# Scan pass of a selective-scan, attention and FFN kernel: named buffers, y stored by pieces, and another order of work

## The chip, the cores and the metric

One core of a Trainium2 chip. The metric is the device time of one execution in microseconds. Before the change the median of three runs is 9894.99 us (9894.46 to 9900.35). The core has five engines that each work through their own list of instructions in order: PE (TensorE, matrix products and transposes into PSUM), DVE (VectorE), ACT (ScalarE), POOL (GpSimd) and SP (SyncE, which here issues almost all DMA transfers). They meet only in semaphores.

## The reference, cut to what matters

Layer 0 is a selective scan over an image of 64 x 64 positions, 8 batches, 192 inner channels, 16 states, run in four directions; layer 1 is an attention without softmax and a quantized feed-forward. The change touches the scan alone:

```python
def step(h, inps):
    d_t, u_t, b_t, c_t = inps
    h = h * jnp.exp(d_t[..., None] * A) + (d_t * u_t)[..., None] * b_t[:, :, None, :]
    y = jnp.einsum('bkdn,bkn->bkd', h, c_t)
    return (h, y)
...
y = out_y[:, 0] + inv_y[:, 0] + wh_y + invwh_y      # the four directions, flipped and transposed back
```

So for each batch, direction k, channel d and state n, `h` is a linear recurrence over 4096 positions; its input is delta x u x B, its decay exp(delta x A), and y sums C x h over the states and then over the directions.

## The kernel before, in words

Three passes run one after the other. The first (normalization, projections, convolution) ends and the second, the **scan pass**, begins at about 683 us; the third (output projection, attention, feed-forward) begins at about 9210 us.

**Tiles of the scan pass.** Batches go in 4 pairs. Each pair has three chunks of 128 partitions: c = 0 and 1 hold 128 channels of one batch (below: wide chunks), c = 2 holds the last 64 channels of both batches (mixed chunks). Each chunk goes through the four directions k, and each direction through 4 pieces of 1024 positions: 16 pieces to a chunk, 192 in all. Directions 2 and 3 run backwards over the positions. A piece has 16 states, and for each state n:

- `decay` (L720): ACT makes `da` = exp(A x delta).
- `products` (L759): the input of the recurrence, a [128, 1024] tile `wide` in PSUM (two of the eight banks), in one of three ways. For states that `WAYS` (L55) gives to ACT, `scaled` (L730) multiplies the transposed `duT` by B on ACT into `x` and PE transposes it into `wide`. For those given to POOL, `scaled_by_pool` (L746) does so on POOL into `xg`. For the rest PE spreads a row of `xb` (B) over the partitions into `wide` and DVE multiplies it in place by `du`.
- `scan` (L783): DVE runs the recurrence from `da` and `wide` into half of a tile `h` (two states to a tile), starting from `carry` unless the piece is the first of its direction.
- `carries` (L807): ACT copies the last column of both halves of `h` for the next piece. `times_c` (L822): POOL multiplies `h` by the loaded rows `c`. `sum_over_n` (L836): PE transposes and adds the terms into `acc` in PSUM.
- Once to a piece, `take_acc` (L878) has ACT copy `acc` into the tile `y`; after the last piece of directions 2 and 3, `store_y` (L894) sends the whole of `y` (4096 positions) to memory. For odd directions each part goes in two transfers.

Around these, `deltas_of` (L645) makes `delta` for two pieces, `prepare` (L596) loads `xb` and `u` and makes `bT`, `du` and `duT`. The projected delta, bT and duT pass through `wide` buffers too: PE fills one, ACT copies it out. `late_x_projection` (L678) and `late_split` (L700) do left-over work of the first pass during the scan.

**What sets the order.** Everything is a Python generator that yields (engine, cost, delay, buffers) before each step. `weave` (L148) is a planner: it keeps a clock for each engine, opens so many units of each kind at once (`room` in its call, L935), and each time emits the step that can begin first by its costs, ties broken by a rank (`at * N + n - lead`, where `lead` is the number in each `add` call). `InOrder` (L85, L93 records every operation) then pins that order on each engine, so the costs decide the order of the instructions, and the chip runs it with its own times. `keep_busy` (L583) adds filler matmuls of a zero tile where the planner sees PE idle.

**Buffers.** The scan pass has 4 `da`, 3 `h`, 4 `x`, 1 `xg`, 6 `c`, 3 `wide` and 1 `acc` buffers (L556). A pool hands its buffers out in turn: the n-th tile of a kind lies in the buffer of the tile n - count before, and waits until that one is released. `Slots` tells the planner the same thing.

Of the kernel before, what the change touches and what calls it, by code (L numbers as in the profile page):

```python
# [42 lines left out]
P = 128  # L43
# [8 lines left out]
NPC = L // T  # L52
NT = T // P

WAYS = [([4, 6, 7, 9, 10, 12, 14, 15], [2, 11]), ([3, 8, 9, 12, 14, 15], [2, 6, 13])]  # L55
NS = 3
SOFT = 2

# [73 lines left out]
class Slots:  # L132
# [5 lines left out]
    def when(self):  # L138
# [2 lines left out]
            return None  # L141
        return 0.0 if self.taken < self.count else self.ends.get(self.taken + 1 - self.count)

    def release(self, which, end):
        self.ends[which] = end


def weave(units, room, finished, between=None):  # L148

    free, clock = {}, 0.0
    waiting = {kind: [u for u in units if u[0] == kind] for kind in room}
    opened, ended, active = {kind: 0 for kind in room}, {kind: set() for kind in room}, []
    while True:  # L160
        for kind, todo in waiting.items():
            while opened[kind] < len(todo) and (opened[kind] < room[kind] or opened[kind] - room[kind] in ended[kind]):
                _, rank, unit = todo[opened[kind]]
                active.append([clock, rank, kind, opened[kind], unit, next(unit)])
                opened[kind] += 1
        best = None
        for at in active:
# [12 lines left out]
        at = best[1]  # L180
        engine, cost, delay = (*at[5], 0.3)[:3]
        if len(at[5]) > 3:
            at[5][3].taken += 1
        clock = best[0][0]
        if between is not None:
            between(engine, clock - free.get(engine, 0.0))
        free[engine] = clock + cost
        at[0] = clock + cost + delay
        try:
            at[5] = at[4].send(at[0])  # L190
        except StopIteration:
            active.remove(at)
            ended[at[2]].add(at[3])
# [47 lines left out]
    return (a_neg, dsum, dt_b, dt_w, sel, sel2), load_dt_w  # L241


def split(engines, pool_of, cost, src, row, rows, pieces, at, dst):

    act, pool, sp = engines
    wide, used = GRP, rows * pieces
    yield "sp", 0.7, 4.0
    bq = pool_of.tile([P, wide], F32, name="bq", tag="late2")
    src = src[row : row + rows].rearrange("r (s t) -> (r s) t", s=pieces)  # L250
    sp.dma_start(bq[0:used], src[:, at : at + wide])
    yield "act", 0.6
    bs = pool_of.tile([P, NS, wide], BF16, name="bs", tag="late")
    act.copy(bs[0:used, 0, :], bq[0:used])
    yield "pool", cost
    pool.tensor_sub(bq[0:used], bq[0:used], bs[0:used, 0, :])
    yield "act", 0.6
    act.copy(bs[0:used, 1, :], bq[0:used])
    yield "pool", cost
    pool.tensor_sub(bs[0:used, 2, :], bq[0:used], bs[0:used, 1, :])  # L260
# [13 lines left out]
def pass1(ctx, tc, g, load_dt_w, ident, mhalf, engines, w_xp, u_d, z_d, xd_d, b_d, dt_d):  # L274
# [254 lines left out]
    for pair in range(NB // 2):  # L529
        batches = (2 * pair, 2 * pair + 1)  # L530
        for b in batches:
            units += [("stats", statistics(b, q)) for q in range(NG)]
            units.append(("norm", group_norm(b)))
            units += [("proj", projection(b, q)) for q in range(NG)]
        for c in ORDER:
            units.append(("conv", convolution(pair, c)))
        for b in batches:
            for o in range(2 if b < LATE_X else 0):
                units += [("xproj", x_projection(b, o, q)) for q in range(NG)]
                if b < LATE:  # L540
                    units += [("split", after(("xd", b, o), split((act, pool, sp), two, 4.4, xd_d[b][o], *w))) for w in splits(b, o, b_d, dt_d)]
    units.append(("later", later_loads()))
    room = {"later": 1, "proj": 4, "norm": 1, "stats": 3, "xproj": 4, "split": 2, "conv": 3}
    weave([(kind, (list(room).index(kind), i), unit) for i, (kind, unit) in enumerate(units)], room, done)
# [3 lines left out]
def pass2(ctx, tc, g, ident, engines, fixed, w_xp, u_d, xd_d, b_d, dt_d, y_d):  # L548
# [5 lines left out]
    two = ctx.enter_context(tc.tile_pool(name="p2two", bufs=2))  # L554
    three = ctx.enter_context(tc.tile_pool(name="p2three", bufs=SOFT + 1))
    room = {"da": 4, "h": 3, "x": 4, "xg": 1, "c": 6, "wide": 3, "acc": 1}  # L556
    slots = {name: Slots(count) for name, count in room.items()}
    pools = {
        name: ctx.enter_context(tc.tile_pool(name=f"p2{name}", bufs=count, **({"space": PSUM} if name in ("wide", "acc") else {})))
        for name, count in room.items()  # L560
    }
    pieces = [
        (pair, c, k, NPC - 1 - i if k >= 2 else i) for pair in range(NB // 2) for c in range(3) for k in range(K) for i in range(NPC)
# [6 lines left out]

    def take(name, shape, dtype=F32):

        return pools[name].tile(shape, dtype, name=name), slots[name].taken

    def one_more(key, of, end):
        counts[key] = counts.get(key, 0) + 1
# [101 lines left out]
    def late_x_projection(b, o, q):  # L678

        yield "scans", 0  # L680
        pair, j = b // 2, b % 2
        cols = slice(q * GRP, (q + 1) * GRP)
        yield "sp", 1.8, 4.0
        ux = one.tile([P, 2, GRP], F32, name="ux", tag="late")
        sp.dma_start(ux[:, 0, :], u_d[b][o][0:P, cols])
        for i in range(2):
            sp.dma_start(ux[64 * i : 64 * i + 64, 1, :], u_d[2 * pair + i][o][P:DI, cols])
        yield "pe", 1.5, 0.2, slots["wide"]
        px, slot = take("wide", [P, T])
        for i, ty in enumerate((0, 1 + j)):  # L690
            pe.matmul(px[:, 0:GRP], w_xp[:, ty, o, :], ux[:, i, :], start=i == 0, stop=i == 1)
        end = yield "act", 0.58, 0.2
        xd = one.tile([P, GRP], F32, name="xd", tag="late2")[0 : 2 * NXD]
        act.copy(xd, px[0 : 2 * NXD, 0:GRP])
        slots["wide"].release(slot, end)
        end = yield "sp", 0.7, 3.0
        sp.dma_start(xd_d[b][o][:, cols], xd)
        one_more(("xd", b, o), NG, end)

    def late_split(b, o, which):  # L700

        yield "scans", 0
        if b >= LATE_X:
            yield "xd", b, o
        yield from split((act, pool, sp), one, 1.25, xd_d[b][o], *which)
        one_more(("split", b), 6, 0.0)

    def load_c(at, m):
# [11 lines left out]
    def decay(at, n):  # L720

        _, c, k, _ = pieces[at]
        yield "delta", at
        end = yield "act", 1.05, 0.2, slots["da"]
# [34 lines left out]
    def products(at, n):  # L759
# [11 lines left out]
        else:  # L771
# [6 lines left out]
            end = yield "dve", 1.22, 0.1  # L778
# [99 lines left out]
    def take_acc(at):  # L878
        pair, c, k, pc = pieces[at]
        o = k % 2  # L880
        yield "sum", at
        end = yield "act", 0.95, 0.1
        if at % (K * NPC) == 0:
            for i in range(2):
                ys[i] = one.tile([P, NBLK, P], F32, name=f"y{i}")
        acc, slot = made["acc"]
        dst = ys[o][:, pc * NT : (pc + 1) * NT, :]
        act.copy(dst, acc)
        slots["acc"].release(slot, end)
        if k >= 2 and at % NPC == NPC - 1:  # L890
            yield "sp", 7.5, 6.0
            store_y(ys[o], o, chunk_rows(pair, c))

    def store_y(y, o, parts):  # L894
        for part, b, ch in parts:
            if o == 0:
                sp.dma_start(y_d[b][0].rearrange("(i p) d -> p i d", p=P)[:, :, ch], y[:, :, part])
            else:

                rows = y_d[b][1].rearrange("(h i w) d -> w h i d", w=2, h=HH)  # L900
                for w in range(2):
                    sp.dma_start(rows[w][:, :, ch], y[w * HH : (w + 1) * HH, :, part])

    units = []
    for at, (pair, c, k, pc) in enumerate(pieces):
# [3 lines left out]
            units.append((kind, at * N + n - lead, unit))  # L909

        if at == 0 or at % SOFT == 1:
            add("soft", 14, deltas_of(at))
        add("prep", 12, prepare(at))
        for n in range(N):
            if n % 2 == 0:
# [7 lines left out]
            add("scan", 0, scan(at, n), n)  # L923
            if n % 2 == 1:
                if at % NPC < NPC - 1:
                    add("carry", 0, carries(at, n // 2), n)
                add("term", -2, times_c(at, n // 2), n)
                add("sum", -6, sum_over_n(at, n // 2), n)
        add("acc", 0, take_acc(at), N)
    late_x = [(b, o, q) for b in range(LATE_X, NB) for o in range(2) for q in range(NG)]  # L930
    late = [("split", 3 * N * (i + 1), late_x_projection(*which)) for i, which in enumerate(late_x)]
    last = [(b, o, w) for b in range(LATE, NB) for o in range(2) for w in splits(b, o, b_d, dt_d)]
    late += [("split", 5 * N * (i + 1), late_split(*which)) for i, which in enumerate(last)]
    units += sorted(late, key=lambda unit: unit[1])
    weave(units, {"soft": 1, "prep": 1, "c": 1, "da": 2, "x": 1, "xg": 1, "dbu": 2, "scan": 2, "carry": 1, "term": 1, "sum": 1, "acc": 1, "split": 1}, done, keep_busy)  # L935


@with_exitstack
# [301 lines left out]
```

## Time and profile before

The profiled execution took 9906.51 us, with a span of 9904.5 us from the first instruction to the last; the median of the timed runs is 9894.99 us.

| engine | busy us | share of the span | what it does most (from the groups of the page) |
|---|---|---|---|
| DVE | 9325.3 | 94% | 3072 scans, 5255.7 + 1703.1 us; 1216 products, 1462.4 us |
| ACT | 9119.9 | 92% | 14336 of x, 4198.0 us; 3072 of da, 3501.1 us |
| POOL | 9004.1 | 91% | 1536 products with c, 6962.1 us at 4554 ns |
| PE | 7951.6 | 80% | sums into acc 3165.9 us, transposes into wide 1523.3 + 495.4 us, filler 1066.0 us |

The granted TensorE clock is 0.963 over the span. One DMA queue carries 2109 MB. The y stores of the page are 8 of 2 MB, 24 of 1 MB and 16 of 512 KB.

How to read it: a busy share is an average over three passes and over both kinds of chunks, which have different limits. Back-to-back instructions of DVE overlap by some 0.085 us in the records, so the mean length of a group (2330 ns for a scan with carry) is longer than the rhythm in which they follow each other. The line L93 is the recording helper's, so instructions are told apart by their tiles.

### The profile page before, as it was taken

What the parts mean: (1) busy time and instruction counts of PE and PEld (TensorE: products, weight loads), DVE (VectorE), ACT (ScalarE), POOL (GpSimd) and SP (SyncE); (2) the same over time, 40 slices, a digit from 0 to 9 for tenths busy, and PEclk for the clock granted to TensorE, in tenths of its full rate; (3) what the DMA queues carried; (4) which work ended last, traced back from release to release, by engine and by line L of the source; (5) the groups of instructions that cost most, each with busy time, mean ns of one, the idle gap of its engine ahead of it and who ended that gap; (6) DMA issues with size and microseconds to landing.
All of it is one profiled execution on the core that took longest, in us unless ns stands there. A gap on an engine that the chain in (4) does not pass through costs nothing.

```text
span 9904.5 us, 162493 instructions
## 1 busy us (share of the span) xinstructions
PE 7951.6 (80%) x57093; PEld 6231.6 (63%) x57093; DVE 9325.3 (94%) x6971; ACT 9119.9 (92%) x21486; POOL 9004.1 (91%) x2911
## 2 busy tenths in 40 slices
PE   7768888888887887888888888878878878878787
PEld 3336666666666666666666666666666666666676
DVE  7879999999999999999999999999999999999687
ACT  5769999999999999999999999999999999999797
POOL 1449999999999999999999999999999999999677
PEclk8889999999999999999999999999999999999898
DMA  5776776789986776799976766899867667999663
GB/s 165 236 224 214 227 238 219 232 216 212 217 225 214 227 228 218 225 219 208 212 227 213 229 222 218 226 209 207 222 218 225 222 213 227 215 209 206 189 185 107
DMA packets 937134, 2120.70 MB, mean 214 GB/s; under 512 B 275371, under 2 KB 423628, under 8 KB 934786
## 3 DMA queue, kind: packets, MB, share of 16 engines
q1 hardware_dynamic: 933514, 2108.96, 76.1%
q8 instruction: 456, 7.47, 0.3%
q14 instruction: 356, 2.92, 0.1%
q0 software_dynamic: 432, 0.94, 0.0%
q10 hardware_dynamic: 2376, 0.40, 0.0%
HBM read 1934.36 MB, written 175.66 MB: 213 GB/s over the span
## 4 chain that ended last, share of the span: by engine, by line
ACT 28%; DVE 25%; issue 19%; PE 11%; POOL 8%; DMA 7%; SPq 1%; DVEq 0%; POOLq 0%; ACTq 0%
DVE h L93 18%; ACT x L93 12%; ACT da L93 10%; POOL c L93 6%; DVE wide L93 5%; PE wide L93 4%; PE acc L93 3%; DMA c<-xd_d 3%; PE pa L93 1%; ACT L93 1%; PE px L93 1%; PE mm L93 1%; DVE u L93 1%; DMA xb<-b_d 1%; ACT y L93 1%
## 5 line engine op out<-in xcount | busy, mean ns | idle before, releaser
L93 POOL TENSOR_TENSOR c<-c,h 128x2048 f32<-128x2048 f32 x1536 | 6962.1, 4554 | 177.7 <-DVE h L93 129.8
L93 DVE TENSOR_TENSOR_SCAN h<-da,carry,wide 128x1024 f32<-128x1024 f32 x2304 | 5255.7, 2330 | 147.7 <-PE wide L93 103.9
L93 ACT ACTIVATE x<-duT,bT 128x128 f32<-128x128 f32 (+1 forms) x14336 | 4198.0, 368 | 13.6 <-PE wide L93 12.3
L93 ACT ACTIVATE da<-delta,a_neg 128x1024 f32<-128x1024 f32 x3072 | 3501.1, 1144 | 139.8 <-DVE h L93 135.6
L93 PE MATMUL acc<-ident,c 128*128 128x128 f32 x24576 | 3165.9, 279 | 380.9 <-POOL c L93 366.7
L93 PEld LDWEIGHTS acc<-ident,c 128*128 128x128 f32 x24576 | 2811.3, 143 | 777.3 <-POOL c L93 649.2
L93 PE MATMUL wide<-ident,x 128*128 128x128 f32 x11264 | 1523.3, 280 | 483.5 <-DVE h L93 449.9
L93 DVE TENSOR_TENSOR_SCAN h<-da,wide 128x1024 f32<-128x1024 f32 x768 | 1703.1, 2268 | 59.0 <-PE wide L93 37.1
L93 PEld LDWEIGHTS wide<-ident,x 128*128 128x128 f32 x11264 | 1268.1, 143 | 768.0 <-DVE h L93 331.9
L93 DVE TENSOR_TENSOR wide<-du,wide 128x1024 f32<-128x1024 f32 x1216 | 1462.4, 1209 | 91.3 <-PE wide L93 66.8
L93 PE MATMUL acc<-sel,zero 96*128 96x512 bf16 x3941 | 1066.0, 380 | 0.0
L93 PE MATMUL wide<-xb,sel 96*128 96x512 bf16 x2432 | 733.2, 386 | 291.8 <-DVE h L93 277.1
L93 POOL TENSOR_TENSOR xg<-duT,bT 128x512 f32<-128x512 f32 (+1 forms) x640 | 892.7, 1409 | 24.1 <-PE wide L93 12.1
L93 PE MATMUL wide<-ident,xg 128*128 128x128 f32 x3584 | 495.4, 284 | 162.4 <-DVE h L93 155.8
L93 PEld LDWEIGHTS <-zero 96*128 96x128 bf16 x3941 | 383.2, 98 | 304.8 <-issue 5.5
L93 PEld LDWEIGHTS wide<-ident,xg 128*128 128x128 f32 x3584 | 416.3, 146 | 249.5 <-issue 149.2
L93 PEld LDWEIGHTS <-sel 96*128 96x128 bf16 x2432 | 220.8, 99 | 458.0 <-issue 226.7
L93 POOL TENSOR_TENSOR du<-delta,u 128x1024 f32<-128x1024 f32 x192 | 457.2, 2381 | 41.2 <-DMA u<-u_d 20.9
L93 DVE SCALAR_TENSOR_TENSOR u<-xpad,conv_w,u 128x4096 f32<-128x4096 f32 x96 | 451.2, 4700 | 1.9
L93 ACT COPY carry<-h 128x2 f32<-128x2 f32 x1152 | 214.4, 186 | 139.9 <-DVE h L93 134.2
L93 POOL TENSOR_TENSOR bq<-bq,bs 128x512 f32<-128x512 f32 (+1 forms) x48 | 120.2, 2506 | 172.1 <-ACT bs L93 163.5
L93 ACT ACT_TABLE_LOAD x196 | 251.5, 1283 | 22.9 <-DMA b2q_raw<-in_b 19.4
(150 smaller groups left out, 6239.5 us busy)
## 6 DMA issues: line engine op xcount, KB each, us to landing
c<-xd_d SPq DMA_DIRECT2D x1024, 1024.0 KB
c<-xd_d SPq DMA_DIRECT2D x1024, 512.0 KB
u<-u_d SPq DMA_DIRECT2D x127, 512.0 KB
xdt<-dt_d SPq DMA_DIRECT2D x1146, 36.0 KB
xb<-b_d SPq DMA_DIRECT2D x382, 96.0 KB
u<-u_d SPq DMA_DIRECT2D x128, 256.0 KB
zs<-z_d SPq DMA_DIRECT2D x128, 256.0 KB
y_d<-y SPq DMA_DIRECT2D x24, 1024.0 KB
```

The costliest lines, as they stand in the source:

```text
L93: ins = getattr(self.engine, op)(*args, **kwargs).ins
```

## The change

The arithmetic stays. What differs:

- Each buffer of the scan pass gets a name of its own (a tag in a pool of one buffer), and the planner's `Buffers` gives a new tile the buffer that comes free first, not the one whose turn it is. The numbers of buffers stay.
- `y` is stored after every piece of directions 2 and 3, a quarter at a time, in place of once after their last piece.
- Other states go to ACT and POOL in `WAYS`, as many as before to each (8 and 2 in wide chunks, 6 and 3 in mixed ones).
- Three products and three scans may be open at once in the planner (two before).
- Ranks: deltas 12 ahead in place of 14, carries 4 later, the copy of acc 2 later. Some costs and delays of the planner are other numbers (da 1.06 for 1.05; late transfers 12 and 25 us for 3 to 4; the delay behind DVE's product 0.0 for 0.1).

```diff
-WAYS = [([4, 6, 7, 9, 10, 12, 14, 15], [2, 11]), ([3, 8, 9, 12, 14, 15], [2, 6, 13])]
+WAYS = [([2, 4, 5, 9, 10, 13, 14, 15], [6, 12]), ([6, 7, 9, 12, 14, 15], [4, 8, 13])]
...
+class Buffers:
+    def __init__(self, count):
+        self.free, self.taken, self.held = [0.0] * count, None, False
+    def when(self):
+        return None if self.held else min((end for end in self.free if end is not None), default=None)
+    def take(self):
+        self.taken = self.free.index(self.when())
+        self.free[self.taken] = None
+    def release(self, which, end):
+        self.free[which] = end
...
-    slots = {name: Slots(count) for name, count in room.items()}
+    slots = {name: Buffers(count) for name, count in room.items()}
     pools = {
-        name: ctx.enter_context(tc.tile_pool(name=f"p2{name}", bufs=count, **({"space": PSUM} if name in ("wide", "acc") else {})))
-        for name, count in room.items()
+        name: ctx.enter_context(tc.tile_pool(name=f"p2{name}", bufs=1, **({"space": PSUM} if name in ("wide", "acc") else {})))
+        for name in room
     }
...
-        return pools[name].tile(shape, dtype, name=name), slots[name].taken
+        which = slots[name].taken
+        return pools[name].tile(shape, dtype, name=name, tag=f"{name}{which}"), which
...
-        yield "sp", 1.8, 4.0
+        yield "sp", 1.8, 12.0
...
-        end = yield "sp", 0.7, 3.0
+        end = yield "sp", 0.7, 25.0
...
-        yield from split((act, pool, sp), one, 1.25, xd_d[b][o], *which)
+        yield from split((act, pool, sp), one, 1.25, 12.0, xd_d[b][o], *which)
...
-        end = yield "act", 0.95, 0.1
+        end = yield "act", 0.95, 3.0
...
-        dst = ys[o][:, pc * NT : (pc + 1) * NT, :]
-        act.copy(dst, acc)
-        slots["acc"].release(slot, end)
-        if k >= 2 and at % NPC == NPC - 1:
-            yield "sp", 7.5, 6.0
-            store_y(ys[o], o, chunk_rows(pair, c))
+        of = slice(pc * NT, (pc + 1) * NT)
+        act.copy(ys[o][:, of, :], acc)
+        slots["acc"].release(slot, end - 3.0)
+        if k >= 2:
+            yield "sp", 3.0, 6.0
+            store_y(ys[o], o, of, chunk_rows(pair, c))
...
-                sp.dma_start(y_d[b][0].rearrange("(i p) d -> p i d", p=P)[:, :, ch], y[:, :, part])
+                sp.dma_start(y_d[b][0].rearrange("(i p) d -> p i d", p=P)[:, of, ch], y[:, of, part])
...
-            add("soft", 14, deltas_of(at))
+            add("soft", 12, deltas_of(at))
...
-                    add("carry", 0, carries(at, n // 2), n)
+                    add("carry", -4, carries(at, n // 2), n)
...
-        add("acc", 0, take_acc(at), N)
+        add("acc", -2, take_acc(at), N)
...
-    weave(units, {"soft": 1, "prep": 1, "c": 1, "da": 2, "x": 1, "xg": 1, "dbu": 2, "scan": 2, "carry": 1, "term": 1, "sum": 1, "acc": 1, "split": 1}, done, keep_busy)
+    weave(units, {"soft": 1, "prep": 1, "c": 1, "da": 2, "x": 1, "xg": 1, "dbu": 3, "scan": 3, "carry": 1, "term": 1, "sum": 1, "acc": 1, "split": 1}, done, keep_busy)
```

More of the change, by code (lines that the diff above doesn't have):

```diff
@@ L142, in when, with take @@
         return 0.0 if self.taken < self.count else self.ends.get(self.taken + 1 - self.count)
+    def take(self):
+        self.taken += 1
     def release(self, which, end):
         self.ends[which] = end
+class Buffers:
[3 more added lines that the diff above has]
+        return None if self.held else min((end for end in self.free if end is not None), default=None)
+    def take(self):
+        self.taken = self.free.index(self.when())
+        self.free[self.taken] = None
+    def release(self, which, end):
+        self.free[which] = end
 def weave(units, room, finished, between=None):
@@ L182, in weave @@
         if len(at[5]) > 3:
-            at[5][3].taken += 1
+            at[5][3].take()
         clock = best[0][0]
@@ L241, in scan_constants, with split @@
     return (a_neg, dsum, dt_b, dt_w, sel, sel2), load_dt_w
-def split(engines, pool_of, cost, src, row, rows, pieces, at, dst):
+def split(engines, pool_of, cost, landing, src, row, rows, pieces, at, dst):
     act, pool, sp = engines
     wide, used = GRP, rows * pieces
-    yield "sp", 0.7, 4.0
+    yield "sp", 0.7, landing
     bq = pool_of.tile([P, wide], F32, name="bq", tag="late2")
@@ L540, in pass1 @@
                 if b < LATE:
-                    units += [("split", after(("xd", b, o), split((act, pool, sp), two, 4.4, xd_d[b][o], *w))) for w in splits(b, o, b_d, dt_d)]
+                    units += [("split", after(("xd", b, o), split((act, pool, sp), two, 4.4, 4.0, xd_d[b][o], *w))) for w in splits(b, o, b_d, dt_d)]
     units.append(("later", later_loads()))
@@ L723, in decay @@
         yield "delta", at
-        end = yield "act", 1.05, 0.2, slots["da"]
+        end = yield "act", 1.06, 0.2, slots["da"]
         da, slot = take("da", [P, T])
@@ L777, in products @@
                 pe.matmul(dbu[:, q : q + GRP], spread(n, c), xb[:, q : q + GRP], start=True, stop=True)
-            end = yield "dve", 1.22, 0.1
+            end = yield "dve", 1.22, 0.0
             dve.tensor_mul(dbu, made[at][2], dbu)
@@ L886, in take_acc, with store_y @@
         acc, slot = made["acc"]
[L887 to L894 removed]
+        of = slice(pc * NT, (pc + 1) * NT)
[4 more added lines that the diff above has]
+            store_y(ys[o], o, of, chunk_rows(pair, c))
+    def store_y(y, o, of, parts):
         for part, b, ch in parts:
             if o == 0:
[L897 removed]
+                sp.dma_start(y_d[b][0].rearrange("(i p) d -> p i d", p=P)[:, of, ch], y[:, of, part])
             else:
@@ L901, in store_y @@
                 for w in range(2):
-                    sp.dma_start(rows[w][:, :, ch], y[w * HH : (w + 1) * HH, :, part])
+                    sp.dma_start(rows[w][:, of, ch], y[w * HH : (w + 1) * HH, of, part])
     units = []
```

## The prediction

> **What bounds the kernel now.** I read the busy shares of the page first, then a table of windows cut at the first scan of each chunk of the scan pass, then the waits of VectorE, then three places in the timeline. The page gives DVE 94%, ACT 92%, POOL 91%, so no share alone says who ends last. The table cut by chunk does; here are two chunks of pair 2, the first of the wide kind (128 channels of one batch), the second of the mixed kind (64 and 64 channels of two batches).
>
> ```profile
> core 0: us, PE busy (x) PEld busy (x) DVE busy (x) ACT busy (x) POOL busy (x), PEclk, DMA share, GB/s
> ...
> 5664.30:6358.60 694.30, 570.38 (x4302) 460.00 (x4300) 681.06 (x353) 657.34 (x1465) 675.64 (x178) 0.98 0.70 221
> 6358.60:7090.10 731.50, 590.08 (x4286) 471.42 (x4285) 700.26 (x369) 716.47 (x1957) 712.28 (x240) 0.96 0.94 211
> ```
>
> A wide chunk is held by DVE (681 of 694 us) with POOL close behind (676); a mixed chunk is held by ACT (716 of 731) with POOL at 712, and its DMA engines are 94% busy against 70%. Summed over the table's twelve rows: the eight wide chunks take 5589.9 us with DVE busy 5450.6 and POOL 5434.4; the four mixed ones take 2935.7 us with ACT busy 2856.8. The change leaves every count of arithmetic instructions as it is, so the most that an order can give in the pass is 139.3 + 78.9 = 218 us.
>
> Who ends DVE's gaps:
>
> ```profile
> DVE h L93 <- PE wide L93: 140.9, 105, 9.7
> DVE wide L93 <- PE wide L93: 66.8, 64, 4.2
> ```
>
> Total us, times, longest: DVE waits for products to arrive in PSUM. There are two kinds of such waits. The first, from the timeline of all engines (start, length, engine, work; in brackets the idle time before and who ended it):
>
> ```profile
> 7897.28 4.56 DVE L93 TENSOR_TENSOR_SCAN h<-da,carry,wide 128x1024 f32<-128x1024 f32 x2
> ...
> 7901.90 1.09 PE L93 MATMUL wide<-ident,x 128*128 128x128 f32 x8 [1.21 <-DVE h L93]
> ...
> 7903.13 2.35 DVE L93 TENSOR_TENSOR_SCAN h<-da,carry,wide 128x1024 f32<-128x1024 f32 x1 [1.28 <-PE wide L93]
> ```
>
> PE could only refill a PSUM buffer when the scan that read it ended at 7901.84, and DVE had no other work ready: 1.09 us of transposes plus two handoffs is the 1.28. I call this a tight refill. Undisturbed, the scan with carry repeats every 2.24 us and the product every 1.11. The second kind, from the DMA queue's timeline and then that of all engines:
>
> ```profile
> 9032.16 8.23 SPq L93 DMA_DIRECT2D y_d<-y  x2
> ```
>
> ```profile
> 9089.29 0.38 PE L93 MATMUL wide<-sel,xb 96*128 96x32 bf16 x8 [7.06 <-DMA xb<-b_d]
> ...
> 9091.59 2.35 DVE L93 TENSOR_TENSOR_SCAN h<-da,carry,wide 128x1024 f32<-128x1024 f32 x1 [9.69 <-PE wide L93]
> ```
>
> Two y stores of 1 MB each enter the queue, the c loads behind them fall due all at once, and 50 us later PE, DVE and ACT (7.00) all stand for one xb load behind that traffic.
>
> **The change, part by part.** The two orders of instructions can be counted without running anything. For each DVE operation I took the PSUM buffer of its product and counted the DVE operations between the one that freed this buffer and itself; the gaps come from the trace of before, as the time beyond the usual overlap of 0.085 us.
>
> 1. Tight refills (nothing between). Wide chunks: 56 before, mean 1.06 us, 59.6 us in all; the new order has 16. That removes 40 x 1.06 = 42.6 us. The naming of buffers is what allows it: before, a new product takes the buffer whose turn it is, now the one that comes free first.
> 2. A scan directly after the product that writes its own input loses 0.20 us (30.6 us over 152 cases in wide chunks); 70 are left: 82 x 0.20 = 16.4.
> 3. One operation between: 689 to 511 cases at 0.031 us: 5.5.
> 4. Against it: delta, bT and duT also pass through these buffers (PE fills, ACT copies out, PE refills). Under the old turn such a buffer came back late. I count refills after such a passage with at most 5.7 us of DVE work to cover it: 38 before, 242 after. The passage of duT takes 1.04 (fill) + 1.00 (copy) + 1.07 (refill) and handoffs of 0.1 each, 3.4 us, that of bT 1.9 to 2.4; against covers of mostly 4.5 and 5.6 it is hidden, with one microsecond of slack. The nearest row: the 38 old ones lost 10.4 us, 0.27 each. So between 0 and 204 x 0.27 = 55 us; I take 15, because 32 of the 38 lost under 0.3.
>
> Wide chunks: -42.6 - 16.4 - 5.5 + 15 = -49.5, leaving 5540 us, in which POOL's 5434 is 98.1%: possible, but near.
>
> 5. y by pieces. In piece 13 of the four mixed chunks DVE stood 6.3, 5.2, 6.6 and 9.7 us, each some 50 us after the stores of one direction's y, and 7.3 us in piece 1 of the first mixed chunk, 60 us after the last stores of the chunk before. Bytes and packet sizes stay; the burst becomes four of a quarter, about 45 us apart. I take 30 of the 35.1 us.
>  The skill speaks against this edit: "DMA: Bandwidth & Descriptors", sections "Anatomy of one DMA" and "Bandwidth", puts about 2.0 us of fixed cost on each DMA and asks for transfers of 1 MiB or more. There are 144 more y stores (192 for 48), of 128 to 512 KB: by the rule an estimate of 144 x 2.0 = 288 us of queue time. The row: SP's queue waits 5686.0 us of the pass for PE to free a c buffer, and nobody but the end of the pass waits for a y store to land. So I count 0 here. Each piece's store now also waits on SP for ACT's copy, with c loads queued behind it; six c buffers are some 27 us of scans, which hides a wait of a few us.
> 6. Mixed chunks: tight refills 20 to 14 at 1.26, own-product scans 61 to 34 at 0.257: 14.5 us. ACT holds these chunks, so I take half, 7.
> 7. Late splits are given 12 and 25 us for their transfers where they had 3 to 4: DVE stood once for such a tile (6.3 us behind POOL's bs). I take 5, between 0 and 15.
> 8. End of the pass:
>
> ```profile
> 9221.65 1.01 ACT L93 COPY y<-acc 128x1024 f32<-128x1024 f32 x1 [20.32 <-PE acc L93]
> 9222.69 7.16 SPq L93 DMA_DIRECT2D y_d<-y  x4
> 9229.89 2.83 SPq L997 DMA_DIRECT2D hmask<-in_head_mask  x1
> ...
> 9233.35 0.40 SPq L93 DMA_DIRECT2D y<-y_d  x1
> ```
>
> The last store takes SP 10.7 us from the copy's end to the first load of the output pass. With a quarter of the bytes, four issues near 0.45 and three of 0.4 us: 3.7. Gain 7.
>
> 9. At nothing: carry copies ranked four later. ACT stands 134 us for them, but in wide chunks ACT has 35 to 40 us spare; the reader of a carry comes a whole piece (about 43 us) later, and h is kept anyway by POOL's product of 4.55 us. If that cover goes, h comes free late and DVE waits. Also at nothing: delta asked for two states later, 155 more filler matmuls on PE (0.38 each, put where PE idles), other states per engine (8 and 2, 6 and 3, as before). ACT gets 113 more separate waits ahead of da: an issue step in the chain is 0.05, so 5.6 us, 2 of them in mixed chunks.
>
> Sum: -49.5 - 30 - 7 - 5 - 7 + 2 = **-97 us**. The profiled span of 9904.5 becomes 9808 (its run, 9906.5, becomes 9810); the median of the runs, 9895.0, lies 11 below that run and becomes 9798.
>
> On the bubbles of the first kind "Perfetto Trace Analysis", "Optimization Strategy", says that a gap repeating on the engine that should be full can mean too few buffers. By that rule nothing of items 1 and 6 would come, since there are three wide buffers before and after: the sum would be -46, 9849. The row says something else: most refills from the same three buffers lose nothing (689 cases with one operation between lost 0.031 each), so the place of the refill in the order decides, and the counts in the new order are what I go by.
>
> **The rivals.** *POOL takes over* (22%): POOL's c products are 4.55 us with 243 us of waits in the pass, 130 of them for DVE's h. If the others stay, DVE's recovered time turns into waits for h buffers, and half of 1 to 3 and of 5 is kept: -50, 9845. For it: POOL is 16 us per chunk from DVE. Against it: the same three h buffers now let many pieces through in 42.6 to 42.8 us, DVE's own work.
> *More than the counts* (20%): all of 5, 6 and 7 and most of the 139 us in wide chunks, since a lost microsecond on DVE also delays ACT and POOL: -155, 9740.
> *Nothing* (5%): gaps are only moved; about 9890.
> *Slower* (7%): item 4 goes wrong. PE and ACT are in-order, so a late ACT copy of duT or delta holds PE at the refill, and the sums behind it hold c buffers and SP. The other items sum to -112; with 242 short refills the kernel is slower once each loses over 0.5 us. At 0.7 each: +169 - 10 - 112 = +47, 9942. For it: one old case of it lost over 4 us. Against it: the slack of a microsecond.
>
> **How the numbers follow.** The forecast has 46%, with 9760 to 9835 as its own range. A difference under 0.2% (20 us) can't be told from none. Range 9715 to 9872: it takes in the first two rivals and leaves out nothing and slower. Faster 88%, same 5%, slower 7%.
>
> **What would show it.** In the profile after: DVE's waits for PE's wide from 208 to about 120 us; the wait of 5 to 10 us in piece 13 of each mixed chunk gone, with xb gone from PE's waits; wide chunks near 692 us on average, mixed ones near 725; SP from the last copy to the first y load under 5 us; ACT's waits for carry mostly gone. I am wrong if DVE's waits move to wide fills that follow duT, delta or bT, or if POOL shows gaps that DVE does not end.

## The result, and the profile after

The changed kernel takes 9725.8 us (median of 4 runs, 9717.4 to 9731.5) against 9897.7 us before on the same chip: ratio 0.9825, 95% interval 0.9808 to 0.9842. That is 172 us, where 97 were forecast. The time lies 34 us beyond the forecast's own range (9760 to 9835) and inside the whole range. The profiled execution has a span of 9728.5 us, 176 less than before. Cut at the first scan of each chunk, as before, its table of windows gives for the same two chunks (time, then busy us of PE, its weight loads, DVE, ACT, POOL, then the granted clock and the DMA share):

```profile
core 0: us, PE busy (x) PEld busy (x) DVE busy (x) ACT busy (x) POOL busy (x), PEclk, DMA share, GB/s
...
5571.40:6252.20 680.80, 563.61 (x4298) 448.46 (x4297) 678.71 (x353) 655.61 (x1463) 675.06 (x177) 1.00 0.73 226
6252.20:6969.90 717.70, 587.15 (x4317) 454.07 (x4316) 699.19 (x370) 710.54 (x1948) 709.97 (x240) 0.99 0.96 215
```

The wide chunk is now DVE's own work: 678.7 of 680.8 us. The mixed chunk is 7 us above ACT's. Summed by kind:

| | before | after | difference | forecast |
|---|---|---|---|---|
| eight wide chunks | 5589.8 | 5474.8 | -115.0 | -49.5 |
| four mixed chunks | 2935.8 | 2891.3 | -44.5 | about -37 |
| from the last scan to the end | 695.4 | 679.5 | -15.9 | -7 |

The waits of DVE, in total us, times and longest, within the scan pass (from 690 us, to leave out its first instructions):

```profile
DVE h L93 <- PE wide L93: 62.1, 45, 5.7
DVE wide L93 <- PE wide L93: 24.7, 26, 1.9
```

and those of ACT:

```profile
ACT da L93 <- DVE h L93: 173.6, 434, 2.1
ACT bT L93 <- PE wide L93: 15.6, 21, 4.2
```

DVE's waits for products fell from 208 to 87 us. Before, ACT's two lines were

```profile
ACT da L93 <- DVE h L93: 135.6, 310, 2.1
ACT carry L93 <- DVE h L93: 134.2, 227, 3.5
```

so the waits in front of carry copies are gone from its list, but those in front of da rose from 136 to 174. POOL's list is led by

```profile
POOL c L93 <- DVE h L93: 54.1, 70, 3.7
POOL du L93 <- DMA u<-u_d: 9.5, 4, 4.5
```

where the first stood at 130 us. So DVE and POOL wait less, ACT's waits for DVE's h fell from 270 to 174 us, and the chain that ended last, as the page gives it by engine, is made of their work:

```profile
ACT 31%; DVE 26%; issue 18%; POOL 10%; PE 10%; DMA 4%; SPq 1%; DVEq 0%; POOLq 0%; ACTq 0%
```

DMA had 7% of it and PE 11% before, ACT 28%, POOL 8%. The end of the pass, from the DMA queue's timeline:

```profile
9060.02 2.70 SPq L93 DMA_DIRECT2D y_d<-y  x4
9062.76 0.64 SPq L1015 DMA_DIRECT2D w_ff<-in_Wff  x1
...
9064.69 0.42 SPq L93 DMA_DIRECT2D y<-y_d  x1
```

The last store keeps SP 2.7 us in place of 7.2, and nothing behind it is held up as hmask was (2.83 us). From the end of ACT's copy (9059.78) to the first y load are 4.9 us in place of 10.7.

### The profile page after: what moved, and what is told of

Read it like the earlier page. It is cut to its first block, busy times and chain, and to the rows that moved or that the text cites. A ratio compares the mean times of both kernels' runs of the same rounds, so it can differ in the third digit from the quotient of the medians.

```text
span 9728.5 us, 163465 instructions
## 1 busy us (share of the span) xinstructions
PE 7918.3 (81%) x57248; PEld 6124.2 (63%) x57248; DVE 9305.7 (96%) x6971; ACT 9101.3 (94%) x21486; POOL 8996.0 (92%) x2911
## 4 chain that ended last, share of the span: by engine, by line
ACT 31%; DVE 26%; issue 18%; POOL 10%; PE 10%; DMA 4%; SPq 1%; DVEq 0%; POOLq 0%; ACTq 0%
DVE h L93 20%; ACT x L93 13%; ACT da L93 11%; POOL c L93 8%; PE wide L93 3%; DVE wide L93 3%; PE acc L93 2%; ACT y L93 1%; PE px L93 1%; PE pa L93 1%; DMA c<-xd_d 1%; ACT L93 1%; ACT duT L93 1%; ACT delta L93 1%; PE mm L93 1%
## 5 line engine op out<-in xcount | busy, mean ns | idle before, releaser
L93 DVE TENSOR_TENSOR_SCAN h<-da,carry,wide 128x1024 f32<-128x1024 f32 x2304 | 5242.4, 2328 | 72.9 <-PE wide L93 37.3
L93 ACT ACTIVATE da<-delta,a_neg 128x1024 f32<-128x1024 f32 x3072 | 3507.1, 1145 | 182.5 <-DVE h L93 173.6
L93 PE MATMUL acc<-ident,c 128*128 128x128 f32 x24576 | 3123.7, 276 | 340.2 <-POOL c L93 332.2
L93 PEld LDWEIGHTS acc<-ident,c 128*128 128x128 f32 x24576 | 2753.0, 141 | 783.5 <-POOL c L93 670.7
L93 PE MATMUL wide<-ident,x 128*128 128x128 f32 x11264 | 1496.9, 277 | 427.6 <-DVE h L93 326.5
L93 PEld LDWEIGHTS wide<-ident,x 128*128 128x128 f32 x11264 | 1246.5, 141 | 697.5 <-DVE h L93 181.7
L93 PE MATMUL acc<-sel,zero 96*128 96x512 bf16 x4096 | 1131.4, 381 | 0.0
L93 PE MATMUL wide<-ident,du 128*128 128x128 f32 x1536 | 205.1, 277 | 85.4 <-DVE h L93 68.2
```

Of the source, the lines that this page charges most:

```text
L93: ins = getattr(self.engine, op)(*args, **kwargs).ins
```

## The experiments

An edit to this kernel changes the planner's view, and the planner then writes another order for everything. So some of these runs keep every other instruction where it stood, and change one thing below the order. The ratios are to the kernel before, on the same chip. That kernel took 9884.5 to 9904.6 us on the chips of these runs, so a time in us can miss or meet an expectation by the chip alone; where it matters, the ratio applied to the 9897.7 us of the result is given beside it. Where a table says "counted", it is the classing of the prediction, made on each run's own trace.

### Naming alone, in the old order

Each tile is placed in the buffer that the new rule gives it, while the planner still reckons with buffers in turn; all five engines have their instructions in exactly the old order.

```diff
+class Both(Slots):
+    def take(self):
+        super().take()
+        self.named.take()
+        self.of[self.taken] = self.named.taken
...
-    slots = {name: Slots(count) for name, count in room.items()}
+    slots = {name: Both(count) for name, count in room.items()}
...
-        return pools[name].tile(shape, dtype, name=name), slots[name].taken
+        which = slots[name].taken
+        return pools[name].tile(shape, dtype, name=name, tag=f"{name}{slots[name].of[which]}"), which
```

> The kernel before with every instruction in its old order on every engine; only which of the same buffers a tile lies in differs (the one free first, by name). Theory A (naming the buffers is the larger part of the gain): tight refills fall from 56 to 8 in wide chunks and from 20 to 7 in mixed ones; 48 x 1.06 + half of 13 x 1.26 = 59 us, and a little from waits that follow delta, bT and duT: 9825 to 9840 us, wide chunks near 691 us. Theory B (the new order, by ranks, open units and states, is the larger part): under 25 us, 9873 or more. Theory C (short refills after delta, bT and duT cost what the tight ones gave): such refills rise from 38 to 127, and the time stays within 20 us of before.

Measured: 9823.0 us, ratio 0.9932 (0.9917 to 0.9947), by ratio 9830. Theory A holds, B and C fall. Here is the place that the prediction showed, piece 2 of the same chunk and the same stretch of the order, on the timeline of all engines:

```profile
7826.93 11.28 DVE L93 TENSOR_TENSOR_SCAN h<-da,carry,wide 128x1024 f32<-128x1024 f32 x5
...
7834.22 0.60 PE L93 MATMUL wide<-xdt,dt_w 108*128 108x512 bf16 x2
7834.66 1.04 PE L93 MATMUL wide<-ident,x 128*128 128x128 f32 x8
...
7838.12 1.21 DVE L93 TENSOR_TENSOR wide<-du,wide 128x1024 f32<-128x1024 f32 x1
```

After the filling for delta (xdt), PE goes straight on to the transposes of x, with no bracket: it writes a buffer that is free already. Before, the same eight transposes stood 1.21 us for a scan, and DVE 1.28 us for them. Now DVE runs five scans without a gap.

The place corrects one thing in what was said of the kernel before: its pool does not keep to a strict turn. There, delta was read out of its own buffer at 7899.91:

```profile
7898.79 1.12 ACT L93 ACTIVATE delta<-wide,dt_b 128x1024 f32<-128x1024 f32 x1
```

In the built program that is the buffer of the tile three before x's, and it was free 2 us before x was filled. Yet x had been given the buffer that the scan was reading until 7901.84; with names it takes the one that delta left. Of the 3661 `wide` tiles of the scan pass, 2980 lie in the buffer of the tile three before, 342 in that of four before, 332 in that of two before and 7 elsewhere, while the planner reckons with three throughout. With a strict turn the same order would have 10 tight refills in wide chunks, not 56. So a part of what naming removes is a pool that departs from what the planner reckons with. A strict turn was not run, and how much of the gain it would bring alone is open.

The same two chunks in the table of windows:

```profile
5620.80:6306.10 685.30, 563.69 (x4302) 452.15 (x4301) 680.60 (x354) 656.20 (x1465) 674.99 (x178) 0.99 0.70 225
6306.10:7035.40 729.30, 583.35 (x4287) 464.55 (x4286) 700.38 (x370) 716.43 (x1957) 712.88 (x240) 0.97 0.94 212
```

The wide one has lost 9 of its 694.3 us and the mixed one 2 of 731.5: ACT's 716 there are untouched, and so are the bursts of y. All wide chunks together go from 5589.8 to 5518.7 us. What the naming took away there, counted in us beyond the usual overlap (number of cases in brackets):

| class in wide chunks | before | naming, old order | both parts, old order | changed kernel |
|---|---|---|---|---|
| tight refill | 59.6 (56) | 11.1 (8) | 11.1 (8) | 16.2 (16) |
| scan after its own product | 30.6 (152) | 30.8 (152) | 30.8 (152) | 12.3 (70) |
| one operation between | 21.5 (689) | 10.8 (625) | 18.2 (625) | 8.7 (511) |
| more between | 16.8 (939) | 29.7 (1084) | 24.4 (1084) | 2.8 (1200) |
| after delta, bT or duT | 37.5 (364) | 12.6 (331) | 14.2 (331) | 14.0 (319) |
| other scans | 1.2 (616) | 1.1 (616) | 0.2 (616) | 1.1 (697) |
| sum | 167.1 | 96.1 | 98.9 | 55.2 |

The second and third runs differ in these chunks by y's stores alone, and single classes still by up to 7 us, so differences of that size within one class say nothing.

### Naming alone, planned with

The same, but the planner knows of it.

```diff
-    slots = {name: Slots(count) for name, count in room.items()}
+    slots = {name: Buffers(count) for name, count in room.items()}
```

> The kernel before with named buffers that the planner also plans with; ranks, states, open units and the y stores are the old ones. Theory A: tight refills 56 to 21 in wide chunks, scans straight after their own product 152 to 56: 35 x 1.06 + 96 x 0.2 = 56 us, and some 15 us in mixed chunks: 9815 to 9840. Theory B: under 25 us, 9873 or more.

Measured: 9810.9 us, ratio 0.9919 (0.9903 to 0.9936), in us just under the range of theory A, by ratio (9818) in it. What planning with the names adds to having them is not clear of the intervals.

### y by pieces alone, planned anew

The kernel before with the new `take_acc` and `store_y`, and all else old.

```diff
-        if k >= 2 and at % NPC == NPC - 1:
-            yield "sp", 7.5, 6.0
-            store_y(ys[o], o, chunk_rows(pair, c))
+        if k >= 2:
+            yield "sp", 3.0, 6.0
+            store_y(ys[o], o, of, chunk_rows(pair, c))
```

> The kernel before with y stored after every piece, all else old. If the burst is what stops DVE in piece 13 of the mixed chunks: those waits (27.8 us, and 7.3 in piece 1 of the first mixed chunk) go and 7 to 16 us come at the end of the pass: 9845 to 9865. Rival (the same bytes only meet other loads later; or the stores hold SP in front of c loads): less than 15 us, 9880 or more.

Measured: 9895.3 us, ratio 1.0004 (0.9995 to 1.0012): nothing, as the rival said. Taken by itself this says that the pieces are worthless. The trace says otherwise: mixed chunks 15 us shorter, the end 17 us shorter, the wide chunks 25 us longer (5614.9), where the counted waits after delta, bT and duT rose from 37.5 to 72.1. The new SP steps had made the planner write another order in chunks where y was never late.

### y by pieces alone, in the old order

The pieces are sent without a step of the planner, so that nothing else moves, but for two memsets on POOL at the end of the pass.

```diff
+        last = at % NPC == NPC - 1
+        if k >= 2 and not last:
+            store_y(ys[o], o, of, chunk_rows(pair, c))
+        if k >= 2 and last:
+            yield "sp", 7.5, 6.0
+            store_y(ys[o], o, of, chunk_rows(pair, c))
```

> The kernel before with y stored after every piece and every other instruction in its old order (on POOL two memsets at the end of the pass change places with the last product). Run e3, where the planner made a new order with the pieces, lost 25 us in the wide chunks to waits that have nothing to do with y. Theory P (the pieces are worth what they remove): the waits of piece 13 in the mixed chunks go (27.8 us) and the end of the pass shortens by 16: 9840 to 9855. Rival Q (the burst isn't what stops DVE there, only the end gains): 9872 to 9882. Rival R (stores ahead of c loads on SP cost as much as they bring): 9885 or more.

Measured: 9867.4 us, ratio 0.9961 (0.9947 to 0.9976). By ratio that is 9859, just above theory P and well below rival Q: more than the end, a little less than all of it. In the profile the mixed chunks are 26 us shorter and the end 20; the wide ones 4 longer. The waits of 5 to 10 us in piece 13 are down to 2.4 in the first mixed chunk and under 2.2 in the other three, but new ones of 7.1 us (piece 10 of the first mixed chunk) and 4.1 us (piece 14 of the last) have come. PE's waits for xb loads fall from 48.5 to 33.1 us and not to nothing (the changed kernel has 17.5, and with whole stores, below, 49.9), but naming alone, with y whole, also brings them to 37.3, so this sum does not separate the two parts. The DMA engines of these chunks are 92% to 96% busy before and 94% to 97% with the pieces, which may leave later loads exposed; that this is the reason is argued, not shown.

### Both in the old order

> The kernel before with both: buffers taken by name, the one free first, and y by pieces; the old order of every other instruction. If the two parts add up: 69 us of e1 and 40 to 50 of theory P: 9770 to 9790, and what the changed kernel has beyond that, some 55 us, belongs to its new order. If the stall only moves (POOL or ACT hold the mixed chunks anyway): 9800 to 9825.

Measured: 9791.7 us, ratio 0.9883 (0.9868 to 0.9897), by ratio 9782: the parts add up. 0.68% and 0.39% add up to 1.07%; measured are 1.17%, the same within the intervals, so the two parts do not get in each other's way. What the changed kernel has beyond this run is its order: 0.58%, some 57 us. In the profiles it is 49.5 us of the wide chunks (the table above: scans straight after their own product 30.8 to 12.3, more between 24.4 to 2.8) and 15 of the mixed ones.

### The changed kernel with buffers in turn

> The changed kernel with buffers handed out in turn again, planned so; states, ranks, three open products and y by pieces stay. Theory A: more than half of the wide chunks' 115 us is lost: tight refills 33 in wide chunks, scans straight after their own product 148: 9800 to 9830. Theory B: it stays near the changed kernel, 9725 to 9755.

The edit undoes `Buffers` and the tags and nothing else. Measured: 9835.2 us, ratio 0.9943 (0.9928 to 0.9958), by ratio 9841, a little worse than theory A said. The wide chunks are at 5574.0, so 99 of their 115 us are lost. Counted as above their sum is 151.1 us, 34.6 of it tight refills and 55.7, the largest class, waits after delta, bT and duT (16.2 and 14.0 in the changed kernel). Mixed chunks (2897.3) and the end (683.4) keep nearly all. So the new order (states, ranks, open units, costs) is worth 16 us in wide chunks without the names, and three times that with them.

### The changed kernel with y stored whole, its order kept

```diff
-            store_y(ys[o], o, of, chunk_rows(pair, c))
+            if at % NPC == NPC - 1:
+                store_y(ys[o], o, slice(0, NBLK), chunk_rows(pair, c))
```

> The changed kernel with its order kept, y stored whole after the last piece of a direction. Theory P: the end of the pass is 16 us longer again and the mixed chunks have their waits of 5 to 10 us back: 9765 to 9780. Rival Q: the end alone, 9738 to 9748.

Measured: 9763.6 us, ratio 0.9855 (0.9841 to 0.9870). That is 30 us by ratio and 38 in us: between rival Q (12 to 22) and theory P (39 or more). The wide chunks are the same (5475.5), the mixed ones 16 us longer, the end 16.

The mixed chunks lose their 16 us in another place than theory P said. In piece 13 of the last three of them no wait of 5 to 10 us comes back, and the first has one of 5.2 us with whole stores and of 5.7 with pieces. Instead DVE stands 3.1, 3.1, 5.4 and 3.1 us in piece 0 of the four mixed chunks, behind the last whole stores of the wide chunk before. In the third of them, from the DMA queue's timeline and then that of all engines:

```profile
6268.41 6.33 SPq L93 DMA_DIRECT2D y_d<-y  x2
6274.86 5.16 SPq L93 DMA_DIRECT2D c<-xd_d  x2
6280.06 1.08 SPq L93 DMA_DIRECT2D xb<-b_d  x2
```

```profile
6290.52 0.37 PE L93 MATMUL wide<-sel,xb 96*128 96x32 bf16 x8 [6.95 <-DMA xb<-b_d]
...
6294.62 4.47 DVE L93 TENSOR_TENSOR_SCAN h<-da,wide 128x1024 f32<-128x1024 f32 x2 [5.35 <-PE wide L93]
```

In the changed kernel the same loads are issued 4 us after y's stores begin, in place of 12, and DVE does not stand for them:

```profile
6263.92 1.27 SPq L93 DMA_DIRECT2D y_d<-y  x2
6266.69 1.27 SPq L93 DMA_DIRECT2D c<-xd_d  x2
6268.01 1.06 SPq L93 DMA_DIRECT2D xb<-b_d  x2
```

So a burst of y stops DVE in either order, but which loads it holds up depends on the order. The end, in the DMA queue:

```profile
9078.22 7.32 SPq L93 DMA_DIRECT2D y_d<-y  x4
9085.59 2.62 SPq L1011 DMA_DIRECT2D w_kv<-in_Wqkv  x1
...
9090.64 0.42 SPq L93 DMA_DIRECT2D y<-y_d  x1
```

The first load of the output pass is issued 23.2 us after the last scan ended, in place of 15.7. That is half of the 16. From this load to the last instruction the pass takes 672.2 us in place of 663.8, but not because its first loads land much later. POOL's first sum on them begins 5.2 us after their issue here, and 4.4 us after it in the changed kernel. First this run, then the changed kernel:

```profile
9096.31 1.80 POOL L93 TENSOR_TENSOR y<-y,yo 128x768 f32<-128x768 f32 x1 [19.58 <-DMA yo<-y_d]
```

```profile
9069.60 1.80 POOL L93 TENSOR_TENSOR y<-y,yo 128x768 f32<-128x768 f32 x1 [11.29 <-DMA yo<-y_d]
```

Up to 560 us after the load this run is at most 2.2 us behind; the rest of the 8 us comes in the last 100 us, where the granted clock is 0.71 against 0.79. What causes it is open, and only 7.5 us of the end are shown to come from the stores.

### States, ranks and open units

Three edits and all of them together, each on the changed kernel and planned anew:

```diff
-WAYS = [([2, 4, 5, 9, 10, 13, 14, 15], [6, 12]), ([6, 7, 9, 12, 14, 15], [4, 8, 13])]
+WAYS = [([4, 6, 7, 9, 10, 12, 14, 15], [2, 11]), ([3, 8, 9, 12, 14, 15], [2, 6, 13])]
...
-                    add("carry", -4, carries(at, n // 2), n)
+                    add("carry", 0, carries(at, n // 2), n)
...
-    weave(units, {"soft": 1, "prep": 1, "c": 1, "da": 2, "x": 1, "xg": 1, "dbu": 3, "scan": 3, "carry": 1, "term": 1, "sum": 1, "acc": 1, "split": 1}, done, keep_busy)
+    weave(units, {"soft": 1, "prep": 1, "c": 1, "da": 2, "x": 1, "xg": 1, "dbu": 2, "scan": 2, "carry": 1, "term": 1, "sum": 1, "acc": 1, "split": 1}, done, keep_busy)
```

> The changed kernel with the old states for ACT and POOL, planned anew. Tight refills are 10 and 9 (changed kernel: 16 and 14), operations with one other in between 731 and 353 (511 and 285), scans straight after their product 65 and 35 (70 and 34). If these counts carry the time, it stays within 15 us of the changed kernel: 9715 to 9745. If the choice of states is a part of the gain of its own: 9750 to 9780.

> The changed kernel with the old rank of the carry copies, planned anew. Theory: a carry copy that ACT reaches before its scan ends holds the da and x behind it; ACT's waits in front of carry (133 us before, 94 in e6, none in the changed kernel) come back and the wide chunks lose 10 to 25 us: 9736 to 9752. Rival: da waits for the same scan anyway (174 us in the changed kernel), so nothing but the name of the wait changes: 9715 to 9733.

> The changed kernel with two open products and scans in the planner. Tight refills 17 and 5 (changed kernel 16 and 14), scans straight after their product 69 and 55 (70 and 34): by the counts at 1.0 and 1.3 us, 0.18 and 0.22 us, the wide chunks stay and the mixed ones gain 7: 9710 to 9730. If the third open product matters by itself: 9745 or more.

> The changed kernel (named buffers in the planner, y by pieces, the new costs) with the old states, two open products and scans, and the old ranks of delta, carry and acc. Run e6 had both parts in the old order at 9792, the changed kernel is at 9726. If planning anew with the names brings most of that step: 9725 to 9745. If the states, the open units and the ranks do: 9765 to 9790.

| on the changed kernel | us | ratio | interval |
|---|---|---|---|
| old states | 9743.0 | 0.9840 | 0.9824 to 0.9857 |
| carries at their old rank | 9731.0 | 0.9843 | 0.9828 to 0.9858 |
| two open products and scans | 9720.0 | 0.9835 | 0.9819 to 0.9851 |
| these three, and delta and acc at their old ranks | 9752.7 | 0.9864 | 0.9849 to 0.9879 |
| none (the changed kernel) | 9725.8 | 0.9825 | 0.9808 to 0.9842 |

By ratio these are 9739, 9742, 9734 and 9763 us. Together they are worth 0.39%, which is clear of the intervals; it lies between the two readings of its expectation, as planning anew with the old knobs accounts for 0.19% of the 0.58% beyond the run with both parts (not clear of the intervals), and the knobs for the rest. No single one is clear of the intervals. The old states stay in the range that the counts gave. For the third open product, its mattering by itself (9745 or more) is not seen, and it is not shown to bring anything. For the carries the time settles neither theory (9731 in us is the rival's, 9742 by ratio the first one's), though the waits moved as the rival says. ACT's in the run with the old rank:

```profile
ACT da L93 <- DVE h L93: 94.7, 248, 2.0
ACT carry L93 <- DVE h L93: 80.3, 177, 1.4
```

94.7 and 80.3 make 175.0, against 173.6 in front of da alone with the new rank: ACT waits for the same scans under another name.

### Left-over work asked for earlier

```diff
-    late = [("split", 3 * N * (i + 1), late_x_projection(*which)) for i, which in enumerate(late_x)]
+    late = [("split", 2 * N * (i + 1), late_x_projection(*which)) for i, which in enumerate(late_x)]
...
-    late += [("split", 5 * N * (i + 1), late_split(*which)) for i, which in enumerate(last)]
+    late += [("split", N * (5 * (i + 1) if i < 6 else 48 + 2.7 * (i - 6)), late_split(*which)) for i, which in enumerate(last)]
```

> The changed kernel with the left-over projections and splits asked for earlier, in the wide chunks: of 16 projections one falls into the first mixed chunk (six in the changed kernel). Mixed chunks are held by ACT and the DMA queue, wide ones have some 25 us of ACT to spare. Theory: the first mixed chunk goes from 740 to about 725, the wide ones lose 3 to 5: 9712 to 9722. Rival: POOL, which has no room in wide chunks, makes them longer by as much: 9725 to 9735.

Measured: 9727.7 us, ratio 0.9840 (0.9825 to 0.9855): no gain. Both halves of the expectation came true: mixed chunks are 18 us shorter together, wide ones 15 longer. The chunk before the first mixed one, and that one:

```profile
1367.40:2064.90 697.50, 580.91 (x4343) 460.06 (x4342) 680.48 (x353) 663.46 (x1476) 682.86 (x183) 0.99 0.72 232
2064.90:2785.90 721.00, 590.70 (x4329) 456.01 (x4327) 698.82 (x369) 715.41 (x1964) 717.58 (x247) 0.99 0.97 217
```

The mixed chunk is at 721 us (740 in the changed kernel), the wide one at 697.5 (684). POOL was busy 682 us of it already in the changed kernel, so the work was moved from a chunk held by ACT and POOL to one held by DVE and POOL. Which waits make up the 15 us between POOL's busy time and the chunk was not followed further.

## Why the prediction was right or wrong

The direction held, and so did its largest cause: DVE waiting for PSUM buffers that the old pool and order gave back late. The size was a little over half of what came: the range as a whole held only because it took in a rival, and the result is 11 us from its end. The term that was most off is step 4, with the sign wrong. By the steps:

1. **Tight refills** in wide chunks: -42.6 forecast, -43.4 counted. Right.
2. **Scans after their own product**: -16.4 forecast, -18.3 counted. Right.
3. **One operation between**: -5.5 forecast, -12.8 counted. The rate itself fell (0.031 to 0.017 us), and I had kept the old one. Why it fell is not shown.
4. **Refills after delta, bT and duT**: +15 forecast, -23.5 counted. This is the step that failed. I saw that such passages now end in quick refills, 242 in place of 38, and carried their old loss over. Those numbers took both kinds of chunks together (163 wide and 79 mixed after, 15 and 23 before), while I booked the cost on the wide ones. In wide chunks the 163 quick ones lost 0.07 us each, and the slow ones, which I had left at their old cost, fell from 30.4 to 2.4 us. Naming in the old order shows it alone: 37.5 to 12.6. In mixed chunks 79 quick refills lost 0.32 each, near my price, but that mean holds one wait of 5.8 us, and 67 of them lost under 0.3.
   To this comes what I had not costed at all: refills with more operations between, 16.8 to 2.8 us. Naming alone did not lessen those (29.7, or 24.4 with y by pieces); the new order removed them. Steps 1 to 4 with these make -112, the wide chunks -115.
5. **y by pieces**: -30 forecast for mixed chunks; -26 with the old order, -16 in the changed kernel. Right in the old order, where the waits of 5 to 10 us in piece 13 went. In the changed order they stay away in three of the four chunks even with whole stores, so there the order removed them; the first mixed chunk keeps waits of 5.1, 4.2 and 5.7 us (pieces 5, 11 and 13). What the pieces save in this order is the wait in piece 0. The other rule weighed there is answered too: 144 more stores of a quarter of the size cost nothing that shows. In the changed kernel storing whole is 0.30% slower, some 30 us. The Trainium skill's advice of large transfers ("DMA: Bandwidth & Descriptors", section "Bandwidth") counts what one transfer achieves; here what counts is what stands behind it. Its figures there, and the 2.0 us of the estimate, are for transfers that GpSimd issues, and these go through SP.
6. **Mixed chunks** by order: -7 forecast. Tight refills and scans after their own product fell by 14.7 us as counted. The largest class was not in the sum: refills with one operation between, which hold the waits of piece 13 too, fell from 65.2 to 13.7 us, and those with more between from 12.4 to 6.3. Against it other waits there (scans whose product had long been made, and refills after bT, delta and duT) grew by 28. The mixed chunks came out at -44.5, of which y's pieces are 16 in this order. In turn and without the names they keep -38.5, so here the gain is the order's and y's more than the names'.
7. **Late splits**: -5 forecast; no run separates it.
8. **The end**: -7 forecast, -15.9 measured. For what the step counted, SP's time from ACT's copy to the first load, it was near: -5.8. Four small issues took 0.68 us each and not 0.45 (and the sum as written there is 3.0, not 3.7). From the end of the last scan to the first load it is -8.5, of which the run with whole stores shows 7.5. The other 7 us lie in the output pass behind it, which the step left out (671.2 us before, 663.8 after). They are not shown to be the stores' doing: they build up in its first 200 us, at a granted clock of 0.82 before and 0.89 after, and in the run with naming alone, which stores y whole, the end is 3.7 us shorter than before too.
9. **At nothing**: carries, states, open units and ranks. Singly not to be told from nothing; together 0.39%, some 38 us, which no item of the sum held.

Of the rivals, "more than the counts" (9740) came nearest. Whether its reason holds, that a microsecond lost on DVE also delays ACT and POOL, no run isolates: in wide chunks the counted gaps alone (-112) give nearly all of the -115. POOL did not take over: its waits for h fell from 130 to 54 us. Of the signs, the wide chunks came to 684 us on average (692 forecast), the mixed ones to 723 (725) and SP to 4.9 us (under 5); xb stays in PE's list with 17.5 us. The rule of repeating gaps ("Perfetto Trace Analysis", section "Optimization Strategy") would have given 9849; the same three buffers, taken in another order, gave 69 us with no instruction moved.

## What to carry to other kernels

A pool that hands out buffers by a rule of its own, and not by which is free, can make a tile wait for a slow holder while another buffer stands empty. Where one kind of buffer serves tiles with very different lives, give each buffer a name and take the one that is free first: no memory is spent, and here even the old order got faster. A large store that nobody waits for can still be the cause of a stall tens of microseconds later: cut it into what one step has produced, and look at the end of the pass, where the next stage's loads stand behind it. And where a planner writes the order, one edit planned anew measures two things; keep the order to measure one.

## What was not expected of the hardware

The granted TensorE clock rose with the shorter runs: 0.963 before, 0.965 and 0.967 with one part, 0.968 with both, 0.976 in the changed kernel, where seven of the eight wide chunks show 1.00, against 0.97 to 0.99 before. The kernel's matmuls are the same but for 155 filler ones. No run separates whether the fuller PE is the reason, and what the clock itself brought is not known.
